# Layer 0's root as a power on GpSimd, for two channel blocks at a time, with order lists for it

## The chip, the cores and the metric

The kernel runs on one core of one Trainium2 chip. The metric is the device time of one execution in microseconds (us); a lower time is better. Engines are named as in the profile: PE (TensorE matmuls), PEld (its weight loads), DVE (VectorE), ACT (ScalarE), POOL (GpSimd), SP (the engine that only issues DMAs here).

## What is computed

Two layers over 32 batches of 512 channels (C) by 1024 columns (N), in float32, with one 512 x 512 matrix `adj`:

```python
q = jnp.einsum('c,bcn->bn', wq, x); k = jnp.einsum('c,bcn->bn', wk, x)
scores = q[:, None, :] + k[:, :, None]
scores = jnp.where(scores > 0, scores, NEG_SLOPE * scores)
att = jax.nn.softmax(scores, axis=-1)
agg = jnp.einsum('bcn,bmn->bcm', x, att)
out = jax.nn.relu(jnp.einsum('oc,bcm->bom', wm, agg) + bm[None, :, None])   # wm = adj
x = _layernorm(x + out, axis=-1)                       # layer 0: (x - m) / sqrt(v + 1e-5)
x = _layernorm(x + einsum('bnf,nm->bmf', x, adj) + bias, axis=-1)           # layer 1
```

## The kernel before

**Attention without the score matrix.** A score depends only on q + k. The kernel ranks the 1024 values of q (`rk`, a comparison with a count, on DVE), counts for each k how many q lie above the threshold (`ct`, a Sign with a sum, on ACT), forms z = adj x (`z`, on PE), scatters the rows of z to DRAM in the order of q (`sc`, indirect DMAs of POOL), loads them back (`sl`, SP), weights them with exponentials (`se`, ACT) and makes running sums from both ends (`u` and `d`, DVE; carries over partitions by `cu`, `cd` on PE, copied by `uc`, `dc` on ACT, added by `tu`, `td` on DVE). That table is written to DRAM (`tw`, `tl`, SP) and each column gathers its row of it (`g`, indirect DMAs of POOL). `mw` (DVE), `ms` (ACT) and `mx` (DVE) mix the two halves of a row; `t` turns the result by PE transposes into channels by columns.

**Layer 0's norm.** The 512 channels are four blocks of 128 partitions. For each block `r` (DVE, line 490) adds relu and residual into `x` with a row sum, and `s0` (ACT, line 468, a Square with a sum) gives the sum of squared deviations. Then one root for all four blocks: `rt` (`root0`, line 500) is a Sqrt on ACT over 128 x 4 values, and `rce` (`root0_end`, line 504) a reciprocal on DVE. `n0` (ACT, line 508) scales each block by it.

**Layer 1** multiplies by adj² + I in a Strassen-like form with seven half-size products: `U`, `V`, `Y`, `Z`, `11`, `12`, `21` (PE, lines 538, 540, 575) for two row groups each, on the sums `t1` to `t4` (DVE). `U` reads blocks 0 and 1 of `x` alone; `11` reads blocks 2 and 3. `Uc`, `Vc`, `Zc`, `ll` (ACT) and `up`, `lr` (DVE) take the products from PSUM; `s1`, `r1`, `n`, `st` are the second norm and the store. `r1` calls `root` (lines 475 and 476), which is on POOL: a multiply-add and a power of -0.5 over 128 x 1 values, followed by line 625.

**Order.** Nothing is scheduled by the compiler. Three lists of words give every engine its order: `head` (once), `loop` (once for each of 14 batches) and `tail` (once). A word is operation, batch relative to the list's base, and block: `rk.-1.5` is ranking of column block 5 of the batch before the base. `emit` (line 657) calls the functions in the order of the words; each engine keeps its own instructions in that order and waits by semaphores. So a word that waits holds up all later words of its engine. `pool_ops` and `pool_last` (lines 654 to 662) make `scatter` put a small memset on POOL between two scatters that follow each other.

**Buffers that tie batches together.** `tab` (the table) and `got` (gathered rows) have one buffer each, `sorted_z` and `table` in DRAM two each, `x` four. `zt`, from which the scatters read, has one, and `t3`, `t4` write into its column blocks 0 to 3. PSUM has four one-bank and two two-bank buffers.

Of the kernel before, what the change touches and what calls it, by code (L numbers as in the profile page):

```python
# [38 lines left out]
AF = mybir.ActivationFunctionType  # L39
# [10 lines left out]
def adj_resnorm_kernel(  # L50
# [447 lines left out]
    def root0(b):  # L498
            v = st[b].v0
            nc.scalar.activation(v[1], v[1], AF.Sqrt, scale=1.0 / N**3, bias=eps)  # L500

    def root0_end(b):
            v = st[b].v0
            nc.vector.reciprocal(v[1], v[1])  # L504
    
# [129 lines left out]
    def store(b, m):  # L635
# [12 lines left out]
        "ms": mix_scale, "mx": mix, "t": turn, "r": residual, "s0": spread0, "rt": root0, "rce": root0_end,  # L648
# [5 lines left out]
    pool_ops = ("sc", "g", "r1")  # L654
# [10 lines left out]
    bias.0 ld.1 ld.2 ld.3 pa.0 z.0.0 pc.0 co.0 zc.0.0 z.0.1 cc.0 ro.0 zc.0.1 pa.1 rc.0 ct.0.1  # L665
    rk.0.1 z.0.2 ct.0.3 rk.0.7 pc.1 rk.0.2 ct.0.5 z.0.4 rk.0.3 ct.0.2 rk.0.4 ct.0.7 rk.0.6 z.0.6
    zc.0.4 zc.0.2 rk.0.0 rk.0.5 co.1 zc.0.6 z.0.5 re.0 cc.1 ct.0.4 oq.0 sc.0.1 sc.0.6 z.0.3
    sc.0.0 zc.0.5 ct.0.6 sc.0.5 sc.0.2 z.0.7 zc.0.3 sc.0.4 ct.0.0 sc.0.3 ro.1 zc.0.7 sc.0.7
    z.1.0 rc.1 rk.1.3 ct.1.6 ct.1.5 rk.1.1 z.1.6 sl.0.0 sl.0.1 rk.1.7 rk.1.5 z.1.2 zc.1.6 rk.1.6
    ct.1.4 rk.1.0 zc.1.0 se.0.0 oq.1 rk.1.2 z.1.4 se.0.1 u.0.0 ct.1.1 ce.0 u.0.1 u.0.2 z.1.1  # L670
    rk.1.4 u.0.3 u.0.4 z.1.5 u.0.5 zc.1.1 zc.1.4 u.0.6 ct.1.3 u.0.7 zc.1.2 ct.1.7 d.0.7 pa.3
    d.0.6 zc.1.5 re.1 d.0.5 sc.1.1 cu.0 pc.3 d.0.4 ct.1.2 sc.1.5 co.3 z.1.3 d.0.3 uc.0 sc.1.2
    cc.3 d.0.2 ct.1.0 tu.0.0 sc.1.0 sc.1.4 z.1.7 d.0.1 zc.1.3 te.0 sc.1.3 d.0.0 tl.0 tu.0.1
    sc.1.6 cd.0 ro.3 dc.0 zc.1.7 pa.2 td.0.0 sc.1.7 z.2.5 rc.3 tw.0.0 rk.3.0 ct.3.0 ct.3.6
    td.0.1 z.2.0 zc.2.5 ct.3.3 ce.1 tw.0.1 rk.3.6 pc.2 ct.3.1 co.2 z.2.4 rk.3.3 ct.3.2 rk.3.1
    ct.3.4 rk.3.4 ct.3.5 z.2.3 cc.2 rk.3.7 zc.2.0 ct.3.7 rk.3.5 g.0.0 sl.1.0 zc.2.4 sl.1.1 ro.2
    rk.3.2 g.0.3 z.2.6 rc.2 g.0.1 ct.2.4 rk.2.2 zc.2.3 z.2.7 rk.2.6 ct.2.0 rk.2.1 we.0 se.1.0
    ct.2.3 rk.2.5 z.2.1 g.0.2 u.1.0 ce.3 g.0.4 u.1.1 oq.2 u.1.2 g.0.6 se.1.1 zc.2.6 rk.2.0 z.2.2
    zc.2.7 g.0.5 ct.2.7 rk.2.3 g.0.7 mw.0.0 rk.2.4 z.3.0 ms.0.2 ms.0.1 mx.0.2 ms.0.0 rk.2.7
    zc.2.1 ms.0.3 ct.2.1 u.1.3 z.3.4 re.2 mx.0.0 sc.2.6 ct.2.2 mw.0.1 sc.2.5 mx.0.1 ms.0.6  # L680
    mx.0.3 we.1 ms.0.5 z.3.1 sc.2.7 mx.0.6 ms.0.7 mx.0.5 ms.0.4 sc.2.4 mx.0.7 zc.2.2 mx.0.4
    sc.2.0 u.1.4 t.0.3 u.1.5 sc.2.3 t.0.1 r.0.3 sc.2.2 zc.3.4 r.0.1 s0.0.3 t.0.2 sc.2.1 u.1.6
    s0.0.1 t.0.0 r.0.2 z.3.2 u.1.7 s0.0.2 r.0.0 zc.3.0 zc.3.1 d.1.7 s0.0.0 cu.1 d.1.6 z.3.3 oq.3
    zc.3.2 d.1.5 uc.1 d.1.4 rt.0 d.1.3 re.3 d.1.2 z.3.5 zc.3.3 rce.0 d.1.1 n0.0.1 sc.3.3 d.1.0
    n0.0.0 sc.3.1 tu.1.0 n0.0.3 cd.1 sc.3.2 t1.0 U.0.0 dc.1 sc.3.0 zc.3.5 td.1.0 n0.0.2 sc.3.5
    U.0.1 ct.2.6 tu.1.1 tw.1.0 Uc.0.0 11.0.0 ct.2.5 td.1.1 11.0.1 Z.0.0 t2.0 tw.1.1 ce.2 V.0.0
    t3.0 Zc.0.0 we.3 t4.0 12.0.0 Uc.0.1 te.1 Vc.0.0 V.0.1 up.0.0 Z.0.1 Vc.0.1 s1.0.0 sl.2.0 tl.1
    Y.0.1 Zc.0.1 sl.2.1 12.0.1 lr.0.1 Y.0.0 up.0.1 se.2.0 g.1.0 u.2.0 21.0.1 lr.0.0 g.1.3 u.2.1
    21.0.0 se.2.1 g.1.1 u.2.2 ll.0.1 s1.0.1 g.1.2 u.2.3 z.3.6 ld.4 u.2.4 ll.0.0 r1.0.1 u.2.5
    ls.0.0 u.2.6 ls.0.1 u.2.7 r1.0.0 s1.0.3 cu.2 d.2.7 zc.3.6 d.2.6 z.3.7 uc.2 mw.1.0 g.1.7  # L690
    d.2.5 ms.1.0 tu.2.0 ms.1.2 g.1.5 n.0.1 g.1.6 pa.4 d.2.4 s1.0.2 tu.2.1 g.1.4 ms.1.3 z.4.5
    n.0.0 sc.3.6 mx.1.0 zc.3.7 r1.0.3 ms.1.1 d.2.3 pc.4 mx.1.2 d.2.2 co.4 z.4.4 mw.1.1 sc.3.4
    d.2.1 ms.1.7 r1.0.2 mx.1.1 ms.1.4 cc.4 ms.1.6 d.2.0 ms.1.5 ro.4 mx.1.4 zc.4.5 mx.1.6 cd.2
    sc.3.7 n.0.2 mx.1.5 z.4.0 mx.1.7 dc.2 st.0.2 rc.4 st.0.0 st.0.1 mx.1.3 ct.4.1 td.2.0 t.1.3
    zc.4.4 ct.4.6 t.1.1 r.1.3 tw.2.0 n.0.3 z.4.1 td.2.1 ct.4.4 zc.4.0 ct.4.5 r.1.1 tw.2.1 t.1.2
    st.0.3 ct.4.2 te.2 t.1.0 rk.4.6 s0.1.1 z.4.2 r.1.2 s0.1.3 r.1.0 s0.1.2 z.4.3 rk.4.4 s0.1.0
    rk.4.0 rt.1 rk.4.1 sl.3.0 tl.2 z.4.7 zc.4.3 sl.3.1 rce.1 rk.4.2 n0.1.1 rk.4.3 zc.4.1 n0.1.0
    rk.4.7 z.4.6 zc.4.2 se.3.0 g.2.0 rk.4.5 g.2.1 t1.1 n0.1.3 U.1.1 g.2.3 u.3.0 n0.1.2 u.3.1
    g.2.2 11.1.1 u.3.2 Uc.1.1 se.3.1 g.2.5 oq.4 u.3.3 we.2 ct.4.3 11.1.0 re.4 g.2.6 u.3.4 zc.4.7
    t2.1 ct.4.0 g.2.4 Z.1.0 u.3.5 ct.4.7 g.2.7 u.3.6 U.1.0 Zc.1.0 sc.4.3 u.3.7 mw.2.0 sc.4.5  # L700
    Z.1.1 d.3.7 ms.2.2 ce.4 sc.4.0 ms.2.1 d.3.6 ms.2.3 12.1.0 mx.2.2 sc.4.1 Zc.1.1 d.3.5 Uc.1.0
    mw.2.1 V.1.0 sc.4.2 d.3.4 ms.2.7 mx.2.1 zc.4.6 V.1.1 Vc.1.0 mx.2.7 up.1.0 12.1.1 Vc.1.1 t3.1
    s1.1.0 up.1.1 Y.1.0 ms.2.5 r1.1.0 ms.2.4 t4.1 ms.2.6 Y.1.1 ms.2.0 lr.1.0 s1.1.1 mx.2.4
    21.1.0 lr.1.1 r1.1.1 mx.2.0 21.1.1 d.3.3 mx.2.6 mx.2.5 cu.3 sc.4.6 ll.1.1 ld.5 d.3.2 n.1.0
    mx.2.3 d.3.1 ll.1.0 t.2.3 uc.3 ls.1.1 ls.1.0 d.3.0 t.2.2 s1.1.2 r.2.3 cd.3 r1.1.2 r.2.2
    t.2.0 dc.3 s1.1.3 tu.3.0 t.2.1 sc.4.7 n.1.2 r.2.0 pa.5 sc.4.4 s0.2.3 st.1.2 td.3.0 st.1.0
    r1.1.3 pc.5 s0.2.2 co.5 r.2.1 z.5.0 tw.3.0 cc.5 s0.2.1 td.3.1 s0.2.0 ro.5 tu.3.1 rt.2 z.5.2
    n.1.1 rc.5 tw.3.1 n.1.3 st.1.1 rce.2 te.3 z.5.1 n0.2.2 rk.5.6 tl.3 st.1.3 n0.2.3 rk.5.5
    n0.2.0 rk.5.3 11.2.0 ct.5.1 rk.5.7 n0.2.1 11.2.1 sl.4.0 rk.5.4 sl.4.1 ct.5.3 U.2.1 g.3.0
    t1.2 zc.5.0 we.4 g.3.2 rk.5.1 U.2.0 g.3.3 rk.5.0 Uc.2.1 ct.5.6 g.3.1 Z.2.0 t2.2 se.4.0  # L710
    zc.5.2 g.3.6 u.4.0 V.2.1 u.4.1 Zc.2.0 g.3.5 ct.5.4 rk.5.2 Z.2.1 g.3.7 Uc.2.0 u.4.2 re.5
    g.3.4 u.4.3 se.4.1 V.2.0 Zc.2.1 oq.5 u.4.4 ct.5.2 sc.5.0 u.4.5 12.2.1 mw.3.0 u.4.6 ms.3.1
    z.5.3 zc.5.1 u.4.7 Vc.2.1 sc.5.1 mx.3.1 ct.5.7 d.4.7 sc.5.2 up.2.1 12.2.0 zc.5.3 d.4.6
    ms.3.3 sc.5.3 mw.3.1 Vc.2.0 z.5.4 up.2.0 ms.3.5 ms.3.0 mx.3.5 ct.5.5 mx.3.3 ms.3.6 t3.2
    ms.3.7 s1.2.0 mx.3.6 Y.2.0 t4.2 zc.5.4 r1.2.0 ms.3.2 mx.3.7 Y.2.1 ms.3.4 lr.2.0 mx.3.2
    21.2.0 mx.3.4 n.2.0 mx.3.0 lr.2.1 t.3.1 s1.2.1 d.4.5 21.2.1 ll.2.0 r.3.1 r1.2.1 ct.5.0 d.4.4
    t.3.0 ld.6 ll.2.1 ls.2.0 d.4.3 t.3.2 s1.2.2 sc.5.4 d.4.2 cu.4 n.2.1 ls.2.1 r1.2.2 r.3.0
    z.5.5 uc.4 st.2.1 d.4.1 st.2.0 s1.2.3 d.4.0 n.2.2 r.3.2 cd.4 st.2.2 tu.4.0 t.3.3 dc.4 s0.3.2
    z.5.6 r.3.3 zc.5.5 s0.3.1 td.4.0 sc.5.5 s0.3.0 pa.6 td.4.1 tw.4.0 s0.3.3 z.5.7 zc.5.6 rt.3
    sc.5.6 r1.2.3 pc.6 rce.3 n0.3.1 co.6 n0.3.0 cc.6 tu.4.1 ro.6 n0.3.3 U.3.0 n0.3.2 t1.3 tw.4.1  # L720
    U.3.1 Uc.3.0 rc.6 zc.5.7 n.2.3 sc.5.7 t2.3 11.3.1 ct.6.2 st.2.3 rk.6.1 Uc.3.1 Z.3.1 ct.6.4
    t3.3 rk.6.3 ct.6.0 V.3.1 ct.6.5 ce.5 te.4 11.3.0 rk.6.0 Vc.3.1 tl.4 sl.5.0 Zc.3.1 sl.5.1
    Z.3.0 oq.6 t4.3 g.4.0 rk.6.6 V.3.0 Zc.3.0 ct.6.6 g.4.6 rk.6.4 12.3.1 Vc.3.0 g.4.2 rk.6.2
    se.5.0 g.4.1 12.3.0 u.5.0 g.4.3 u.5.1 Y.3.0 g.4.4 rk.6.7 z.6.1 g.4.5 up.3.0 g.4.7 up.3.1
# [238 lines left out]
```

## Time and profile before

| what | value |
|---|---|
| median of 3 runs | 2062.61 us (2061.65 to 2064.26) |
| profiled execution: time, span of its instructions | 2065.32 us, 2063.6 us |
| PE busy | 2004.7 us, 97% of the span |
| DVE, ACT, POOL busy | 1674.9, 1496.3, 874.6 us (81, 73, 42%) |
| granted TensorE clock, mean | 0.991 |
| line 500 on ACT: table loads, Sqrt | 31 x 1283 ns, 32 x 297 ns |
| line 298 on ACT: table loads ahead of the Exp | 26 x 1283 ns |
| line 504 on DVE, reciprocal of 128 x 4 | 32 x 177 ns (median) |
| lines 475 and 476 on POOL, 128 x 1 (mean) | 362 and 743 ns |

Busy time counts when an engine works, not whether the work sets the end. A matmul's end is modelled and overlaps the next one's start, so PE's pace is read from the distance of starts: 47 matmuls of `z` (128 x 512 outputs each) fill 20.33 us in the timeline, 0.43 us each.

### The profile page before, as it was taken

The page shows a single profiled execution, that of the slowest core. Times are in us where ns is not written, and L with a number is a line of the kernel's source. Part 1 is how long each engine was busy: PE and PEld are TensorE (multiplying, and loading weights), DVE is VectorE, ACT ScalarE, POOL GpSimd, SP SyncE. Part 2 cuts the span into 40 slices and gives each one's busy share as a digit, 9 for nine tenths or more (in the row PEclk, how much of TensorE's full clock was granted, in tenths as well). Part 3 has the DMA queues.
Part 4 walks back from the last instruction along what each step waited for, and adds up shares of the span by engine and source line. Part 5 has one row for each costly group of instructions (what it writes and reads, how often), then busy time and mean ns, then how long its engine had stood idle before and what let it go on. Part 6 is the DMA issues. An engine that isn't in the chain of part 4 may idle for free. (4 is left out here: it accounts for less than half of the span.)

```text
span 2063.6 us, 22066 instructions
## 1 busy us (share of the span) xinstructions
PE 2004.7 (97%) x6609; PEld 956.7 (46%) x6609; DVE 1674.9 (81%) x2778; ACT 1496.3 (73%) x2560; POOL 874.6 (42%) x1106
## 2 busy tenths in 40 slices
PE   8999999999999999999999999999999999999976
PEld 4444444444444444444444544444444444444432
DVE  6888898798877889887889888789778888789672
ACT  3566787678776777777777777777777777767566
POOL 4344543344343444443444443453444443443421
PEclk9999999999999999999999999999999999999988
DMA  5558776866667766667766767766677766677752
GB/s 226 212 222 312 275 287 266 306 264 257 271 245 291 307 255 246 271 266 292 306 241 250 273 268 296 290 249 258 255 276 306 276 244 268 245 269 273 286 204 82
DMA packets 137967, 541.04 MB, mean 262 GB/s; under 512 B 14404, under 2 KB 14416, under 8 KB 129656
## 3 DMA queue, kind: packets, MB, share of 16 engines
q1 hardware_dynamic: 80464, 337.47, 41.2%
q0 software_dynamic: 57344, 202.15, 26.0%
q8 instruction: 52, 0.85, 0.2%
q14 instruction: 67, 0.55, 0.1%
q10 hardware_dynamic: 40, 0.02, 0.0%
HBM read 270.29 MB, written 269.29 MB: 261 GB/s over the span
## 5 line engine op out<-in xcount | busy, mean ns | idle before, releaser
L310 PE MATMUL z_ps<-adj_t,x 128*128 128x512 f32 x2048 | 906.6, 593 | 0.4 <-ACT zt L316 0.4
L310 PEld LDWEIGHTS z_ps<-adj_t,x 128*128 128x128 f32 x2048 | 384.1, 190 | 448.0 <-issue 439.5
L324 POOL DMA_INDIRECT sorted_z<-zt,to x256 | 377.2, 1473 | 481.0 <-ACT zt L316 403.7
L432 POOL DMA_INDIRECT got<-table,of x256 | 262.2, 1024 | 209.6 <-issue 87.8
L271 DVE SCALAR_TENSOR_TENSOR junk_v<-qb,qkc,tie 128x1024 uint8<-128x1024 f32 x256 | 328.2, 1282 | 4.0
L284 ACT ACTIVATE junk_s<-qb,qkc 128x1024 bf16<-128x1024 f32 x256 | 293.9, 1148 | 18.9 <-DVE qb L261 17.0
L475 POOL TENSOR_SCALAR var<-var 128x1 f32<-128x1 f32 x128 | 46.3, 362 | 461.9 <-ACT junk L468 458.6
L454 ACT ACTIVATE got<-got,w 128x512 f32<-128x512 f32 x256 | 172.2, 713 | 64.2 <-DVE w L449 56.6
L316 ACT COPY zt<-z_ps 128x512 f32<-128x512 f32 x256 | 144.4, 577 | 68.4 <-PE z_ps L310 63.2
L459 DVE SCALAR_TENSOR_TENSOR got<-got,w 128x512 f32<-128x512 f32 x256 | 180.9, 745 | 10.9 <-ACT got L454 10.7
L490 DVE SCALAR_TENSOR_TENSOR x<-agg_ps,nbm,x 128x1024 f32<-128x1024 f32 x128 | 161.4, 1280 | 23.1 <-PE agg_ps L482 22.7
L372 DVE SCALAR_TENSOR_TENSOR tab<-tab,ac 128x513 f32<-128x513 f32 x224 | 168.0, 750 | 3.0
L631 ACT ACTIVATE g<-g,nb,var 128x1024 f32<-128x1024 f32 x128 | 157.8, 1238 | 11.8 <-POOL nb L625 11.8
L468 ACT ACTIVATE junk<-g,tot 128x1024 bf16<-128x1024 f32 x128 | 146.6, 1146 | 21.3 <-DVE g L595 16.8
L362 DVE SCALAR_TENSOR_TENSOR tab<-tab,ac 128x514 f32<-128x514 f32 x192 | 144.5, 752 | 16.9 <-ACT ac L348 11.7
L468 ACT ACTIVATE junk<-x,tot 128x1024 bf16<-128x1024 f32 x128 | 146.8, 1147 | 13.6 <-DVE x L490 8.3
L405 DVE TENSOR_TENSOR tab<-tab,carry 128x2052 f32<-128x2052 f32 x64 | 144.8, 2292 | 11.5 <-ACT carry L387 11.5
L540 PE MATMUL sum_ps<-x,adj 128*128 128x512 f32 x256 | 131.4, 637 | 16.3 <-ACT x L508 16.3
L482 PE MATMUL agg_ps<-ident,got 128*128 128x128 f32 x1024 | 133.4, 278 | 11.2 <-issue 4.7
L508 ACT ACTIVATE x<-x,var 128x1024 f32<-128x1024 f32 x128 | 138.5, 1149 | 0.7 <-DVE var L504 0.6
L601 DVE SCALAR_TENSOR_TENSOR g<-sum_ps,g 128x512 f32<-128x512 f32 x64 | 44.0, 687 | 111.8 <-ACT junk_s L284 75.3
L482 PEld LDWEIGHTS agg_ps<-ident,got 128*128 128x128 f32 x1024 | 115.2, 143 | 36.3 <-DVE x L490 12.2
(121 smaller groups left out, 2698.8 us busy)
## 6 DMA issues: line engine op xcount, KB each, us to landing
table<-tab SPq DMA_DIRECT2D x64, 2056.0 KB
tab<-sorted_z SPq DMA_DIRECT2D x64, 1028.0 KB
x<-in_x_dram SPq DMA_DIRECT2D x128, 512.0 KB
out_dram<-g SPq DMA_DIRECT2D x128, 512.0 KB
sorted_z<-zt,to POOLq DMA_INDIRECT x256
got<-table,of POOLq DMA_INDIRECT x256
adj_in<-in_adj_dram SPq DMA_DIRECT2D x1, 1024.0 KB
table<-end SPq DMA_DIRECT2D x32, 2.0 KB
```

Source lines behind the costliest of these rows:

```text
L271: nc.vector.scalar_tensor_tensor(junk, s.qb, s.q[:, j : j + 1], tie[:, at : at + N], ALU.subtract, ALU.is_gt, accum_out=s.rank[:, j : j + 1],)
L284: nc.scalar.activation(junk, s.qb, AF.Sign, bias=s.k[:, j : j + 1], accum_out=s.sign[:, j : j + 1])
L310: nc.tensor.matmul(s.z[j], xt[:, c, j * P : (j + 1) * P], adj_t[:, c, :], start=(c == 0), stop=(c == CT - 1),)
L324: nc.gpsimd.indirect_dma_start(out=sorted_z[b % 2][:, :], out_offset=bass.IndirectOffsetOnAxis(ap=s.to[:, j : j + 1], axis=0), in_=zt[:, j ...
L372: nc.vector.scalar_tensor_tensor(v, v, c, s.zs[:, j + 1, 0:D], ALU.mult, ALU.add)
L432: nc.gpsimd.indirect_dma_start(out=s.got[:, j, :], out_offset=None, in_=table[b % 2][:, :], in_offset=bass.IndirectOffsetOnAxis(ap=s.of[:, ...
L454: nc.scalar.activation(down, down, AF.Copy, scale=s.w[:, 1, j : j + 1])
L459: nc.vector.scalar_tensor_tensor(up, up, s.w[:, 0, j : j + 1], down, ALU.mult, ALU.add)
L468: nc.scalar.activation(junk, t, AF.Square, bias=v[0][:, i : i + 1], scale=-float(N), accum_out=v[1][:, i : i + 1],)
L482: nc.tensor.transpose(s.agg[o][:, j * P : (j + 1) * P], s.got[:, j, o * P : (o + 1) * P], ident)
L490: nc.vector.scalar_tensor_tensor(t[:, o, :], s.agg[o], nbm[:, o : o + 1], t[:, o, :], ALU.max, ALU.add, accum_out=s.v0[0][:, o : o + 1],)
L631: nc.scalar.activation(g, g, AF.Identity, bias=s.nb[:, m : m + 1], scale=s.v1[1][:, m : m + 1])
```

## The change

The root of layer 0's norm leaves ACT and DVE. `rt` now takes a half, h = 0 for blocks 0 and 1 or h = 1 for blocks 2 and 3, and calls the `root` that layer 1 has: two POOL instructions over 128 x 2 values. `rce` is gone. There are 64 words `rt` in place of 32 `rt` and 32 `rce`; all other words are the same, 5600 in all, but all three lists are new in their order. The loop begins at another point of the cycle, so `head` reaches one batch further and the loop still runs 14 times. `rt` joins the operations that reset the memset rule of POOL.

```diff
-    def root0(b):
-            v = st[b].v0
-            nc.scalar.activation(v[1], v[1], AF.Sqrt, scale=1.0 / N**3, bias=eps)
-
-    def root0_end(b):
-            v = st[b].v0
-            nc.vector.reciprocal(v[1], v[1])
-    
+    def root0(b, h):
+        root(st[b].v0, slice(2 * h, 2 * h + 2))
+
...
-        "ms": mix_scale, "mx": mix, "t": turn, "r": residual, "s0": spread0, "rt": root0, "rce": root0_end,
+        "ms": mix_scale, "mx": mix, "t": turn, "r": residual, "s0": spread0, "rt": root0,
...
-    pool_ops = ("sc", "g", "r1")
+    pool_ops = ("sc", "g", "r1", "rt")
...
-    for b in range(12, B - 6):
+    for b in range(13, B - 5):
```

Of the lists, the part of the loop around the root (before, then after):

```diff
-    r.-3.1 pa.0 uc.-2 r.-3.3 sc.-1.0 t.-3.0 pc.0 n.-4.2 d.-2.2 co.0 r1.-4.3 t.-3.2 te.-2 s0.-3.3
-    st.-4.2 d.-2.1 z.-1.4 r.-3.2 s0.-3.1 sc.-1.2 cc.0 r.-3.0 s0.-3.2 sc.-1.3 tu.-2.0 z.-1.5
-    s0.-3.0 sc.-1.1 zc.-1.4 d.-2.0 n.-4.3 sc.-1.4 tu.-2.1 rt.-3 st.-4.3 cd.-2 z.-1.6 dc.-2
-    rce.-3 zc.-1.5 td.-2.0 n0.-3.1 sc.-1.5 n0.-3.2
...
+    d.-2.3 r1.-4.3 r.-3.1 s0.-3.0 t.-3.2 n.-4.0 tu.-2.0 z.-1.3 zc.-1.2 st.-4.0 pc.0 r.-3.2
+    sc.-1.2 d.-2.2 sc.-1.0 co.0 zc.-1.3 z.-1.4 cc.0 d.-2.1 n.-4.1 sc.-1.3 te.-2 s0.-3.1 st.-4.1
+    d.-2.0 st.-4.2 tu.-2.1 n.-4.3 rt.-3.0 cd.-2 st.-4.3 t.-3.3 dc.-2 tl.-2 zc.-1.4 ro.0 td.-2.1
+    s0.-3.2 sc.-1.4 z.-1.7 r.-3.3 tw.-2.1 rc.0 s0.-3.3 z.-1.5 td.-2.0 n0.-3.1 rt.-3.1 ct.0.6
+    rk.0.0 tw.-2.0 n0.-3.0 z.-1.6 rk.0.3 zc.-1.5 we.-2 sc.-1.5 n0.-3.2 rk.0.7 rk.0.2 U.-3.1
```

The last root of the tail (batch 31 is -1), before and after:

```diff
-    mx.-1.5 s1.-2.2 up.-2.1 t.-1.1 ll.-2.1 s1.-2.1 t.-1.3 r.-1.1 r1.-2.1 r.-1.3 s0.-1.1 t.-1.0
-    r.-1.0 s0.-1.3 t.-1.2 r1.-2.2 r.-1.2 s0.-1.0 ls.-2.1 s0.-1.2 r1.-2.0 rt.-1 s1.-2.3 rce.-1
-    n0.-1.1 r1.-2.3 n0.-1.0 n.-2.0 t1.-1 U.-1.1 n0.-1.3 st.-2.0 U.-1.0 n0.-1.2 t2.-1 11.-1.0
...
+    mx.-1.7 n.-2.0 ls.-2.0 t.-1.0 up.-2.1 s1.-2.2 st.-2.0 r.-1.0 t.-1.1 s1.-2.1 r.-1.1 t.-1.3
+    s0.-1.0 r1.-2.1 r.-1.3 s0.-1.1 t.-1.2 Y.-2.1 r.-1.2 s0.-1.3 rt.-1.0 s0.-1.2 lr.-2.1 21.-2.1
+    n0.-1.1 rt.-1.1 n0.-1.0 ll.-2.1 r1.-2.2 U.-1.1 t1.-1 n0.-1.2 n0.-1.3 U.-1.0 n.-2.2 t2.-1
```

The stretch of the tail where batch 31's table is finished (-1) and batch 30's residual is made (-2), before and after:

```diff
-    d.-1.0 t.-2.0 tu.-1.0 s1.-3.1 st.-3.2 t.-2.1 cd.-1 r1.-3.1 r.-2.0 n.-3.0 dc.-1 ls.-3.1
-    r.-2.1 t.-2.2 s0.-2.0 td.-1.0 t.-2.3 n.-3.1 s0.-2.1 st.-3.1 r.-2.2 tw.-1.0 tl.-1 r.-2.3
-    s0.-2.2 td.-1.1 s0.-2.3 rt.-2 tu.-1.1 s1.-3.3 rce.-2 tw.-1.1 r1.-3.3 n0.-2.0 st.-3.0 n0.-2.1
...
+    td.-1.1 t.-2.0 n.-3.2 t.-2.1 st.-3.2 r.-2.0 tw.-1.1 r.-2.1 t.-2.2 s0.-2.0 tu.-1.0 s0.-2.1
+    t.-2.3 n.-3.3 rt.-2.0 td.-1.0 r.-2.2 n0.-2.0 tw.-1.0 r.-2.3 s0.-2.2 te.-1 s0.-2.3 tl.-1
+    st.-3.3 n0.-2.1 rt.-2.1 st.-3.1 U.-2.1 t1.-2 n0.-2.3 U.-2.0 g.-1.0 n0.-2.2 g.-1.2 t2.-2
```

And in the head, where batch 1's gathered rows are turned (`t.1`), before and after:

```diff
-    n.0.0 sc.3.6 mx.1.0 zc.3.7 r1.0.3 ms.1.1 d.2.3 pc.4 mx.1.2 d.2.2 co.4 z.4.4 mw.1.1 sc.3.4
-    d.2.1 ms.1.7 r1.0.2 mx.1.1 ms.1.4 cc.4 ms.1.6 d.2.0 ms.1.5 ro.4 mx.1.4 zc.4.5 mx.1.6 cd.2
-    sc.3.7 n.0.2 mx.1.5 z.4.0 mx.1.7 dc.2 st.0.2 rc.4 st.0.0 st.0.1 mx.1.3 ct.4.1 td.2.0 t.1.3
...
+    mx.1.7 r1.0.1 ms.1.0 mx.1.6 uc.2 ls.0.1 pa.4 mx.1.0 ms.1.5 d.2.2 sc.3.4 mx.1.5 n.0.1 z.4.4
+    mx.1.2 sc.3.6 n.0.0 d.2.1 st.0.1 mx.1.4 pc.4 st.0.0 s1.0.3 d.2.0 tu.2.1 t.1.1 r1.0.3 co.4
+    cd.2 cc.4 r.1.1 t.1.0 dc.2 zc.4.4 sc.3.7 r.1.0 n.0.3 t.1.3 z.4.0 td.2.1 st.0.3 s0.1.0 s0.1.1
```

## Prediction

> **What bounds the kernel now.** I read the page's busy shares and slices first.
>
> ```profile
> PE 2004.7 (97%) x6609; PEld 956.7 (46%) x6609; DVE 1674.9 (81%) x2778; ACT 1496.3 (73%) x2560; POOL 874.6 (42%) x1106
> ...
> PE   8999999999999999999999999999999999999976
> ...
> PEclk9999999999999999999999999999999999999988
> ```
>
> PE is full in 38 of 40 slices; its clock falls only in the last two. The busy time by stretch says how much is left (stretch, its length, then busy us of PE, PEld, DVE, ACT, POOL, the clock, DMA share, GB/s):
>
> ```profile
> 0.00:60.00 60.00, 51.44 (x197) 25.19 (x198) 40.14 (x76) 23.88 (x43) 25.40 (x38) 1.00 0.60 228
> ...
> 130.00:200.00 70.00, 66.48 (x215) 31.29 (x214) 54.54 (x79) 43.63 (x76) 32.73 (x32) 0.98 0.74 286
> ...
> 500.00:1700.00 1200.00, 1196.38 (x3956) 571.88 (x3955) 997.70 (x1657) 899.45 (x1537) 526.57 (x653) 1.00 0.69 271
> ...
> 1960.00:2000.00 40.00, 26.45 (x74) 13.54 (x73) 27.21 (x33) 26.46 (x39) 15.15 (x20) 0.79 0.57 220
> 2000.00:2040.00 40.00, 33.29 (x96) 15.07 (x95) 20.53 (x39) 28.80 (x44) 4.03 (x12) 0.91 0.24 97
> 2040.00:2063.60 23.60, 11.28 (x26) 4.47 (x24) 4.18 (x10) 11.45 (x17) 4.02 (x12) 0.81 0.22 89
> ```
>
> In 1200 us of loop PE is idle for 3.6 us. In the last 104 us it is idle for 32.6. The page Perfetto Trace Analysis of the Trainium skill (Identifying the Most-Contended Engine) calls matmul busy share a poor measure, because matmuls overlap; so I checked starts: `z` matmuls follow each other at 0.43 us, transposes at 0.11, and a loop period of 62.2 us (starts of `row`) holds about 60.9 us of such distances. What is above them is mostly changes of operand, and some 0.4 us of `t` waiting for the last `mx`. The loop is PE's and has no slack to give; only the ends have. PE's waits after 1880 us:
>
> ```profile
> PE sum_ps L540 <- ACT x L508: 16.3, 3, 8.8
> ```
>
> Those are `U` waiting for `n0` of batches 29, 30 and 31, so the root stands on this path there and nowhere else.
>
> **What the change removes.** The groups of the root:
>
> ```profile
> L476 POOL TENSOR_TENSOR var<-var,power 128x1 f32<-128x1 f32 x128 | 95.2, 743 | 10.7
> ...
> L475 POOL TENSOR_SCALAR var<-var 128x1 f32<-128x1 f32 x128 | 46.3, 362 | 461.9 <-ACT junk L468 458.6
> ...
> L500 ACT ACT_TABLE_LOAD x31 | 39.8, 1283 | 0.5
> ...
> L298 ACT ACT_TABLE_LOAD x26 | 33.4, 1283 | 0.4
> ...
> L500 ACT ACTIVATE var<-var,eps 128x4 f32<-128x4 f32 x32 | 9.5, 298 | 0.4
> ...
> L504 DVE RECIPROCAL var<-var 128x4 f32<-128x4 f32 x32 | 5.6, 176 | 13.4 <-ACT var L500 13.0
> ```
>
> The page ScalarE: Activation LUTs (What ACT_TABLE_LOAD costs) gives 1283 ns for a load, and a drain of about 1380 ns with it. The trace agrees on the load to the ns and shows no drain: below, the Sqrt starts 0.02 us after its load ends. Sqrt and Exp take turns, so each brings the other's load back: 31 + 26 + 4 (line 348) loads, of which one stays. ACT loses 60 x 1.28 + 9.5 = 86 us, DVE 5.6. That all loads go with Sqrt I take as given: no other pair of functions causes one now.
>
> **What it adds.** 64 pairs on POOL. The trace has only 128 x 1; two columns can't cost less than the fastest (0.18 + 0.55 us) nor more than two single ones (2 x 1.10 mean), so 0.73 to 2.2 us a pair; I take 1.15, 74 us in all, on an engine that is idle for 58% of the time. The spread is real (0.55 to 2.67 us for the power); GPSIMD Engine Reference (Key points) says that POOL shares its SBUF interfaces with DVE, which fits the slow ones lying beside busy DVE. No DMA is added; each moved word takes its DMAs with it on SP and POOL.
>
> **In the loop I cost this at nothing.** What covers it: counting PE's work along the new list, `rt.0` stands 9.4 us of PE work ahead of `n0.1`, and `n0.0` 3.4 us ahead of `U`; `rt.1` stands 3.5 us ahead of `n0.2`, and `n0.3` 2.3 us ahead of `11`. Queued behind a waiting `rt.1` on POOL are the next batch's scatters from block 5 on; but `zc.5`, which they need, comes 4 us later still. Before, `rt` had 4.3 us to `n0` and 4.3 from there to `U`, and PE did not wait. ACT's 2.7 us a period becomes idle time, since PE sets the period. The gathers stand 14 us ahead of `mw` in place of 8.5, and all but one `mx` 3 us ahead of `t`, so some of the 0.4 us may go: I take -2 us over some 20 periods, from -7 to +5.
>
> **In the tail it pays.** The path of batch 31 in the profile before, ACT first, then DVE, then POOL:
>
> ```profile
> 1979.32 1.28 ACT L500 ACT_TABLE_LOAD   x1
> 1980.62 0.30 ACT L500 ACTIVATE var<-var,eps 128x4 f32<-128x4 f32 x1
> ...
> 2019.75 0.30 ACT L500 ACTIVATE var<-var,eps 128x4 f32<-128x4 f32 x1
> ```
>
> ```profile
> 1980.02 2.29 DVE L405 TENSOR_TENSOR tab<-tab 128x2052 f32<-128x2052 f32 x1
> 1982.23 0.17 DVE L504 RECIPROCAL var<-var 128x4 f32<-128x4 f32 x1
> ```
>
> ```profile
> 1989.40 1.85 POOL L432 DMA_INDIRECT got<-table,of  x1 [6.04 <-DMA table<-tab]
> ```
>
> DVE works without pause from 1953 until the last table add ends at 1982.2; then write (7.2 us), gathers, mix (last `mx` 2011.7), four residuals, four `s0` (until 2019.7), Sqrt, reciprocal, two `n0`, and `U`'s real matmuls at 2023.3.
>
> Step a, DVE: between `mw.30.0` and the last table add of batch 31 the new list has all the same words but `te.31` (0.7), `up.29.0` (1.2), `lr.29.0` (0.7) and the residuals of blocks 2 and 3 (2 x 1.28): -5.2 us. `mw.30.0` needs the fifth gather in place of the fourth: +1.3. The table is ready at 1978.3, -3.9.
>
> Step b: the gathers start at 1985.5 and the last `mx` is done at 2007.8. PE can't take `t.31` sooner than its own work allows: `U.30.1` stays near 1983.4 (residual 3 now ends at 1980.8, then `s0` and one `n0`), and 22.6 us of products lie between, plus 2.5 at half clock, so 2008.5. Both arrive together.
>
> Step c: `U` reads blocks 0 and 1, whose root is now done beside `s0` of 3 and 2. From the last `s0` to the first `n0` there were 1.4 us (Sqrt, reciprocal, an `s1`); now none. `U.31.1` at 2018.2 in place of 2023.3: -5.1.
>
> Step d: `Y.30.1` and `21.30.1` (3.4 us) are moved into this gap, which shrinks from 6.2 us of idle time to pieces of about 1.3. TensorE: Matmul & The Clock Gate (What's actually happening) has the clock halved after an idle window of about 3.4 us; the trace agrees: the clock was 0.58 from 2023 to 2028, after that gap, which cost 2.1 us. That goes: -2.1. `12.31.1` now stands between `Y.31.1` and `21.31.1`, where PE waited 0.95 us for `lr`: -0.9. At the very end `s1.31.1` falls ahead of `ll.31.1`: +0.6. Tail: -5.1 - 2.1 - 0.9 + 0.6 = -7.5, from -10 to -3 (only the 1.4 of step c and half of d).
>
> **In the head it costs.** Before, PE waited 3.4 us at 176 us (`co.4`, behind ACT's wait for gathers) and then ran at half clock (1.7). Now `t.1.1`, the first word that needs all of batch 1's mix, stands after 161 us of PE work in place of 170. Its data is not earlier: `t.0` comes 10 us later, so DVE's residuals and with them batch 1's last table add end near 147 in place of 143.7, and gathers start near 163 (160.05 before). Eight gathers without a `r1` between them save 4 us, so `mw.1.1` stays near 180 and the last `mx` near 187. PE arrives at 176 and waits 11 us, plus 2.3 at half clock, against 5.1: +8. Later waits between 229 and 350 us (4.7 us in all) came from PE running ahead of DVE, and shrink: -5. Head: +3, from -2 to +9.
>
> **The sum.** -7.5 - 2 + 3 = -6.5 us on the profiled execution's 2065.3 (span 2063.6), which lies 2.7 above the median of 2062.6: 2056.
>
> **Rivals.** (1) The freed ACT time helps the loop too, and `t`'s wait ends: 22 periods x 0.35 = 7.7 in place of 2, giving 2050. For it speaks the longer lead of gathers and `mx`; against it that PE waits so little. (2) The head's wait is not given back, and the table of batch 31 is no earlier, so that the tail gives only its lower bound: +8 - 3 - 2 = +3, 2065.6. For it speaks that every step of the head's path is a wait seen before; against it that DVE set the pace there and PE's place in its list then matters little. (3) Slower: POOL's order. If `s0.3` slips in the loop by more than the 4 us that `zc.5` leaves, `rt.1` holds the scatters of blocks 5 to 7, and the table load behind them, which already ends waits of ACT line 348 (67.5 us in 34 times). Each us beyond 4 then lengthens 20 periods; it decides from 0.55 us a period (+11 against -6.5). At 0.7 it gives 2070. Against it: ACT has 2.7 us more room than before, and POOL waits for ACT 404 us at the scatters today.
>
> **How the numbers follow.** A change of under 0.2% (4.1 us) can hardly be told from none here. The forecast has 0.55 (2056, own range 2051 to 2061), rival 1 0.18, rival 2 0.16, rival 3 0.11. Faster than 2058.5: 0.8 of the forecast, all of rival 1, a little of 2: 0.64. Slower than 2066.7: 0.11. The rest, 0.25, lies between. The range 2047 to 2066 leaves out rival 3 and the far ends of rivals 1 and 2.
>
> **What would show it.** Right: one or two table loads; PE idle under 5 us from 500 to 1700; batch 31's first gather 3 to 5 us nearer to the end of its PE work, and no half clock after the last root; a PE wait of some 10 us near 176. Wrong: PE idle in every period with POOL named, or a tail whose last gather is no earlier against batch 31's last `z`.

## The result and the profile after

The changed kernel takes **2058.46 us** (median of 18 runs, 2055.18 to 2061.96); the kernel before, in 18 runs on the same chip, 2062.90 (2060.07 to 2066.96). The ratio is 0.998, with a 95% interval of 0.9973 to 0.9987: 4.4 us, about 0.2%. The same kernel measured twice more as a base of the experiments gave 0.9962 (0.9949 to 0.9976) and 0.9987 (0.9981 to 0.9994), so the three measurements give a gain of 4.4, 7.8 and 2.6 us, and what differs from one to the next is about as large as the gain.

The profiled execution took 2055.65 us (span 2053.8). It is one of the quickest, as that of before (2065.32) is one of the slower ones: the two profiles are 9.7 us apart, the medians 4.4. So a profile shows here where time went; how much of it is in an ordinary run the medians say.

From the page after, PE's busy share, its slices and its clock:

```profile
PE 2003.1 (98%) x6609; PEld 956.0 (47%) x6609; DVE 1673.3 (81%) x2746; ACT 1405.8 (68%) x2467; POOL 1029.1 (50%) x1182
...
PE   8999999999999999999999999999999999999967
...
PEclk9999999999999999999999999999999999999989
```

ACT lost 90.5 us, GpSimd (POOL) gained 154.5. The half clock is in one slice instead of two. The busy time by stretch (stretch, length, busy us of PE, PEld, DVE, ACT and POOL, clock, DMA share, GB/s):

```profile
130.00:200.00 70.00, 63.86 (x225) 31.15 (x224) 55.60 (x79) 44.09 (x77) 33.45 (x38) 0.93 0.71 271
...
500.00:1700.00 1200.00, 1200.00 (x3971) 573.77 (x3970) 1003.13 (x1646) 847.10 (x1489) 636.32 (x698) 1.00 0.71 274
1960.00:2000.00 40.00, 27.58 (x75) 13.66 (x76) 28.83 (x39) 25.30 (x37) 22.69 (x24) 0.75 0.68 264
2000.00:2040.00 40.00, 38.34 (x111) 17.37 (x110) 19.05 (x35) 29.02 (x44) 7.89 (x19) 1.00 0.13 53
```

PE has no idle time at all in 1200 us of loop (3.6 before). From 2000 to 2040 it is busy for 38.3 us in place of 33.3, at full clock in place of 0.91. From 130 to 200 it is busy for 63.9 in place of 66.5: the head got worse. The groups of the root, shapes kept apart:

```profile
L475 POOL TENSOR_SCALAR var<-var 128x2 f32<-128x2 f32 x64 | 86.8, 1356 | 85.4 <-ACT junk L468 84.5
L476 POOL TENSOR_TENSOR var<-var,power 128x2 f32<-128x2 f32 x64 | 78.0, 1218 | 5.3
...
L163 ACT ACT_TABLE_LOAD x1 | 1.3, 1283 | 4.5 <-DVE zero L137 4.5
```

One table load is left. A pair of the root takes 1.36 + 1.22 = 2.57 us.

To add up the waits of PE by place I took, from the trace, every distance between the starts of two matmuls that is over 0.13 us above what that kind takes when nothing waits (0.43 us for 512 columns, 0.11 for a transpose). Half clock is in it. Differences of the sum agree with differences of the spans within about 2 us:

| kernel (its profiled time) | to 300 us | 300 to 480 | 480 to 1700 | 1700 to 1920 | from 1920 | sum |
|---|---|---|---|---|---|---|
| before (2065.3) | 12.6 | 2.6 | 4.6 | 2.4 | 32.8 | 54.9 |
| after (2055.7) | 21.3 | 0 | 0 | 0.3 | 24.6 | 46.2 |

So in the profiles the tail gives 8.2, the loop 6.7, and the head costs 6.1. PE's waits in the tail, from 1880 us on:

```profile
PE carry_ps_False L380 <- ACT junk L468: 9.0, 1, 9.0
PE sum_ps L535 <- ACT x L503: 5.6, 2, 4.2
```

The 16.3 us of `U` for three batches are 5.6 for batch 30 alone; a wait of 9.0 us stands at `cd.31` instead. The profile puts it down to ACT, but what `cd.31` reads is DVE's last `d` of batch 31, which ends at 1965.5, 0.1 us before the matmul starts. The columns of a timeline line are start, duration, engine, line, operation, and what was waited for. The path of batch 31, first DVE's last table add, then the first gather, then ACT's last `s0` and the first `n0`:

```profile
1974.38 2.29 DVE L405 TENSOR_TENSOR tab<-tab,carry 128x2052 f32<-128x2052 f32 x1
```

```profile
1984.00 1.05 POOL L432 DMA_INDIRECT got<-table,of  x1 [2.11 <-DVE x L514]
```

```profile
2012.29 1.15 ACT L468 ACTIVATE junk<-x,tot 128x1024 bf16<-128x1024 f32 x1
2013.35 0.19 ACT L468 ACTIVATION_READ_ACCUMULATOR junk<-x,tot 128x1 f32 x1
2013.44 2.17 ACT L503 ACTIVATE x<-x,var 128x1024 f32<-128x1024 f32 x2
```

`n0` starts when the last `s0` ends, `U` of batch 31 follows at 2015.7 (its small bias matmul at 2015.2), and from the end of `t.31` to its last matmul at 2040.9 PE has one wait of more than 0.2 us, of 0.95.

### The profile page after: what moved, and what is told of

The parts are those of the page before. It is cut to its first block, busy times and chain, and to the rows that moved or that the text cites. A ratio compares the mean times of both kernels' runs of the same rounds, so it can differ in the third digit from the quotient of the medians.

```text
span 2053.8 us, 22188 instructions
## 1 busy us (share of the span) xinstructions
PE 2003.1 (98%) x6609; PEld 956.0 (47%) x6609; DVE 1673.3 (81%) x2746; ACT 1405.8 (68%) x2467; POOL 1029.1 (50%) x1182
## 4 chain that ended last, share of the span: by engine, by line
PE 91%; DVE 3%; ACT 2%; DMA 2%; issue 1%; POOL 1%; SPq 0%; ACTq 0%; DVEq 0%; POOLq 0%
PE z_ps L310 41%; PE sum_ps L535 21%; PE pair_ps L535 11%; PE pair_ps L570 5%; PE agg_ps L482 5%; PE qk_ps L221 3%; PE q_tp L252 1%; PE carry_ps_False L380 1%; PE carry_ps_True L380 1%; DMA x<-in_x_dram 1%; PE pair_ps L533 1%; PE sum_ps L533 1%; ACT junk L468 1%; DVE tab L405 1%; DVE junk_v L271 0%
## 5 line engine op out<-in xcount | busy, mean ns | idle before, releaser
L324 POOL DMA_INDIRECT sorted_z<-zt,to x256 | 352.9, 1378 | 284.1 <-ACT zt L316 166.4
L475 POOL TENSOR_SCALAR var<-var 128x1 f32<-128x1 f32 (+1 forms) x192 | 144.4, 752 | 567.9 <-ACT junk L468 563.0
L490 DVE SCALAR_TENSOR_TENSOR x<-agg_ps,nbm,x 128x1024 f32<-128x1024 f32 x128 | 162.9, 1278 | 37.3 <-PE agg_ps L482 37.1
L476 POOL TENSOR_TENSOR var<-var,power 128x1 f32<-128x1 f32 (+1 forms) x192 | 180.1, 938 | 16.0
L503 ACT ACTIVATE x<-x,var 128x1024 f32<-128x1024 f32 x128 | 144.9, 1143 | 18.7 <-POOL var L476 18.5
L590 DVE SCALAR_TENSOR_TENSOR g<-pair_ps,g 128x1024 f32<-128x1024 f32 x64 | 78.2, 1221 | 82.8 <-PE pair_ps L535 60.4
```

The source lines that it names most:

```text
L324: nc.gpsimd.indirect_dma_start(out=sorted_z[b % 2][:, :], out_offset=bass.IndirectOffsetOnAxis(ap=s.to[:, j : j + 1], axis=0), in_=zt[:, j ...
L476: nc.gpsimd.tensor_tensor(v[1][:, at], v[1][:, at], power[:, at], ALU.pow)
```

## The experiments

All were timed against the kernel before on their own chip, so they are compared by their ratio to it. The sums of PE's waits, as above, each from one profiled execution:

| kernel | ratio, interval | to 300 | 300 to 480 | 480 to 1700 | 1700 to 1920 | from 1920 |
|---|---|---|---|---|---|---|
| changed, again | 0.9962 (0.9949, 0.9976) | 19.5 | 0 | 0 | 0 | 25.1 |
| changed, third time | 0.9987 (0.9981, 0.9994) | 21.0 | 0 | 0 | 0 | 25.2 |
| operation alone | 1.0127 (1.0107, 1.0146) | 13.1 | 3.6 | 29.5 | 3.6 | 33.7 |
| operation moved up | 1.0166 (1.0136, 1.0196) | 13.7 | 5.2 | 30.0 | 7.8 | 34.0 |
| order alone | 0.9986 (0.9979, 0.9994) | 23.7 | 0 | 3.5 | 1.6 | 24.8 |
| loads back | 0.9978 (0.9970, 0.9985) | 19.6 | 0 | 1.6 | 1.9 | 25.1 |
| new tail alone | 0.9985 (0.9977, 0.9994) | 12.0 | 3.6 | 2.2 | 4.6 | 25.7 |
| old tail | 1.0018 (1.0006, 1.0030) | 20.9 | 0 | 0 | 0 | 35.0 |
| old head | 0.9953 (0.9939, 0.9967) | 13.2 | 5.4 | 0 | 1.0 | 25.6 |
| old head with Sqrt | 0.9956 (0.9944, 0.9969) | 13.9 | 5.6 | 0.2 | 1.4 | 25.3 |
| root doubled | 1.0050 (1.0037, 1.0063) | 30.4 | 0 | 3.2 | 2.4 | 26.6 |
| root in one piece | 1.0123 (1.0108, 1.0138) | 29.8 | 1.0 | 12.3 | 2.1 | 29.6 |

**The changed kernel again.** 

> The changed kernel once more, as the base for the other three and for a second profile, since its single times spread over 7 us (2055 to 2062) around 2058.5 and the first profile (2055.65) is one of the quickest. Expected: 0.998 of the kernel before. Theory: an ordinary execution shows the same head and tail, and now and then the wait of `t` for the last `mx` in the loop, as the kernel before does, with some 3 us in all. Rival: the 3 us lie in the head or in the tail, so that one of the two gains read from the first profile is partly luck.

2057.88 us (2054.26 to 2062.27, 7 runs). Its profile came from its quickest run and again shows no wait in the loop; neither does the third one, of an execution of 2056.39. No profile is of one of the longer executions, so where those lose up to 8 us is open. One hint: in each of the three measurements of this kernel the executions with a mean granted clock of 0.988 or 0.989 took longer on average than those with 0.990 or 0.991 (2059.9 against 2057.7 us, 2060.7 against 2056.5, 2060.5 against 2057.9), so more time at half clock is part of it.

**Operation alone.** The lists of before; only this:

```diff
     def root0(b):
-            v = st[b].v0
-            nc.scalar.activation(v[1], v[1], AF.Sqrt, scale=1.0 / N**3, bias=eps)
+        for h in range(2):
+            root(st[b].v0, slice(2 * h, 2 * h + 2))
     def root0_end(b):
-            v = st[b].v0
-            nc.vector.reciprocal(v[1], v[1])
+        pass
-    pool_ops = ("sc", "g", "r1")
+    pool_ops = ("sc", "g", "r1", "rt")
```

> The order of the kernel before, with only the operation changed: the two pairs of columns of the root on GpSimd at the word `rt`, no Sqrt, no reciprocal. Theory (the order pays, the operation is hidden): ACT gives up 86 us of table loads that PE did not wait for; in the tail a load, a Sqrt and a reciprocal (1.76 us) are replaced by four GpSimd instructions (2.2 to 4.4 us), so 0 to +4 us, about 2064. Rival (the operation pays, the lists only follow it): ACT's 2.7 us a period end the waits of `t` and the tail gains, so about 2058, the whole of what the change brought.

2093.13 us, 27 us slower than before: outside both expectations. Of the 28.5 us that PE waits more, 24.9 lie between 480 and 1700; the waits from 500 to 1700 us:

```profile
PE sum_ps L539 <- ACT x L507: 23.2, 17, 1.8
```

`U` waits for `n0` in 17 periods. One of them, on POOL, then ACT, then DVE:

```profile
934.66 2.57 POOL L324 DMA_INDIRECT sorted_z<-zt,to  x1 [0.23 <-issue]
937.30 1.89 POOL L475 TENSOR_SCALAR var<-var 128x2 f32<-128x2 f32 x1
939.28 2.66 POOL L476 TENSOR_TENSOR var<-var,power 128x2 f32<-128x2 f32 x1
942.02 0.19 POOL L475 TENSOR_SCALAR var<-var 128x2 f32<-128x2 f32 x1
942.30 0.70 POOL L476 TENSOR_TENSOR var<-var,power 128x2 f32<-128x2 f32 x1
```

```profile
931.95 1.15 ACT L468 ACTIVATE junk<-x,tot 128x1024 bf16<-128x1024 f32 x1
...
941.97 4.28 ACT L507 ACTIVATE x<-x,var 128x1024 f32<-128x1024 f32 x4 [4.67 <-POOL var L476]
```

```profile
934.11 2.29 DVE L405 TENSOR_TENSOR tab<-tab 128x2052 f32<-128x2052 f32 x1
936.85 4.50 DVE L405 TENSOR_TENSOR tab<-tab,carry 128x2052 f32<-128x2052 f32 x2 [0.45 <-ACT carry L387]
```

The last `s0` ends at 933.1, the first `n0` starts 8.9 us later. In the kernel before, in the period around 927 us, this stretch is 4.2 us, and the root in it is a table load of 1.28, a Sqrt of 0.30 and a reciprocal of 0.18. The 8.9 us are two parts of about the same size: until 937.2 POOL is at scatters that stand ahead of the root, and the first pair then takes 4.6. Each of the first three POOL instructions shown ends 0.1 to 0.8 us after a table add of DVE does; the second pair, behind the adds, takes 0.19 + 0.70. Over this whole trace the power on two columns takes 2.71 us (median) beside a table add with the carry and 0.70 where DVE is idle. The Trainium skill, SBUF — State Buffer (Who interferes with whom), says that a VectorE instruction with two inputs in SBUF contends with a GpSimd instruction that reads SBUF, and calls such contention an exclusive lock. The traces agree: in the changed kernel's, a pair that lies beside `L490`, which has one of its inputs in PSUM, keeps its 0.19 and 0.72 us.

**Operation moved up.** As in operation alone, but `rt.b.h` stands right behind the later of the two `s0` of its half:

```diff
-... s0.15.2 sc.17.3 tu.16.0 z.17.5 s0.15.0 sc.17.1 ... sc.17.4 tu.16.1 rt.15
+... s0.15.2 rt.15.1 sc.17.3 tu.16.0 z.17.5 s0.15.0 rt.15.0 sc.17.1 ... sc.17.4 tu.16.1
```

> The old order with the root on GpSimd, as in the run that lost 27 us, but each pair of the root stands right behind the later of its two `s0`, ahead of the scatters that it stood behind. In that run's trace, at 933.1 us the last `s0` is done; GpSimd then does a scatter until 937.2, the first pair of the root until 941.9 (4.6 us, beside DVE's table add), and the first `n0` starts at 942.0. Theory (the place in GpSimd's queue is the loss): the first `n0` comes 4 us sooner or more, `U`'s wait of 1.0 to 1.8 us in each period goes, and the time falls to 0.997 to 1.000 of before. Rival (the length of the pair beside the table adds is the loss): the pairs move into the other table add, half of the loss stays, 1.004 to 1.008.

2093.32 us, no better (the profile is of a longer execution, 2100.04); both expectations fell, the theory's by most. POOL and DVE in one period:

```profile
938.25 1.57 POOL L475 TENSOR_SCALAR var<-var 128x2 f32<-128x2 f32 x1 [1.26 <-ACT junk L468]
939.90 1.12 POOL L476 TENSOR_TENSOR var<-var,power 128x2 f32<-128x2 f32 x1
941.21 2.37 POOL L324 DMA_INDIRECT sorted_z<-zt,to  x1 [0.20 <-issue]
943.66 1.89 POOL L475 TENSOR_SCALAR var<-var 128x2 f32<-128x2 f32 x1
945.63 2.66 POOL L476 TENSOR_TENSOR var<-var,power 128x2 f32<-128x2 f32 x1
```

```profile
938.01 1.76 DVE L405 TENSOR_TENSOR tab<-tab 128x1539 f32<-128x1539 f32 x1
...
940.35 2.29 DVE L405 TENSOR_TENSOR tab<-tab 128x2052 f32<-128x2052 f32 x1
943.20 4.50 DVE L405 TENSOR_TENSOR tab<-tab,carry 128x2052 f32<-128x2052 f32 x2 [0.56 <-ACT carry L387]
```

The run did not do what it was made for. In this order the half that `U` needs (blocks 0 and 1) is the second pair, and the scatter that I had wanted behind the root stands between the two. From the last `s0` (939.3) to the first `n0` (948.3) it is 9.0 us again: 4.3 for the rest of the other half's pair and the scatter, 4.6 for the pair itself. From 938 to 948 POOL does about one instruction for each table add of DVE, the scatter too. So both runs show that a root next to a row of table adds, with `n0` and `U` right behind, costs some 30 us; how much of it is the place in the queue and how much the longer pair is not settled.

**Order alone.** The new lists with Sqrt and reciprocal by halves:

```diff
     def root0(b, h):
-        root(st[b].v0, slice(2 * h, 2 * h + 2))
+        v = st[b].v0[1][:, 2 * h : 2 * h + 2]
+        nc.scalar.activation(v, v, AF.Sqrt, scale=1.0 / N**3, bias=eps)
+    def root0_end(b, h):
+        v = st[b].v0[1][:, 2 * h : 2 * h + 2]
+        nc.vector.reciprocal(v, v)
```

> The lists of the changed kernel, but the root by Sqrt on ACT and a reciprocal on DVE, for two blocks at a time at the words `rt` (the reciprocal one DVE word later), so the table loads come back, some 60 of them. Theory (the order pays): 2058.5 plus 1 to 2 us for the load and Sqrt in the tail, about 2060, faster than the kernel before. Rival (the operation pays): 2062 or more.

2061.46 us against 2057.88 for the changed kernel on the same chip and 2065.72 before: about half of that gain is there without the new operation. The changed kernel's other two ratios, 0.998 and 0.9987, are as good as the 0.9986 here, so by them all of it is. What the operation adds to the order is between nothing and 4 us. The tail is the same (24.8 against 25.1 of waits); the profile is of one of the longer executions (2065.74).

**Loads back.** The changed kernel with an unused Sqrt:

```diff
         root(st[b].v0, slice(2 * h, 2 * h + 2))
+        if h == 0:
+            nc.scalar.activation(look, eps[0:1, :], AF.Sqrt)
```

> The changed kernel with a Sqrt of a single element on ACT at each first half of the root, used by nobody: it brings the table loads back (two a batch, about 2.6 us of ACT), while the root stays on GpSimd. The new lists with the old Sqrt and reciprocal stood 3.6 us above the changed kernel (medians). Theory (ACT's time is hidden, as the prediction has it): 0 to 1 us above the changed kernel; the 3.6 us then belong to the chain Sqrt, reciprocal on DVE, norm. Rival: the loads are what those 3.6 us were: 3 to 4 us above.

0.9978, between the three ratios of the changed kernel. By the profile, PE waits 2 to 4 us more in all; from 480 to 1920, where the changed kernel has almost none, it waits 3.5. Two loads a batch are hidden but for about that; the two theories are not told apart.

**New tail alone, and old tail.** The lists are cut at word 4978 and go on with the words left over in the other kernel's order, with that kernel's root.

> The kernel before, with its Sqrt and its order up to word 4978 (batch 27's norm), then the changed kernel's order and root for the last four batches. It measures the tail's part alone. Theory: the steps a to d of the tail hold, 7 to 8 us under the kernel before (0.9963); the waits of `U` for the root of batch 31 and the half clock go. Rival: the tail's gain is only there behind the new loop, because DVE's backlog at the cut decides: then under 3 us.

> The reverse: the changed kernel up to word 4978, then the order and the Sqrt of before for the last four batches. Theory: what is left is the loop's gain (7 us of waits of `t` by the profiles) less the head's cost (5 to 6 us), so 0 to 3 us under the kernel before (0.999). Rival: loop and head bring nothing and the two results of this pair add up with all of it in the tail: 1.000 here and 0.996 for the new tail alone.

The new tail alone: 2061.98 us, 3 us under before; its interval, about 1 to 5 us, leaves out the 7 to 8 of the theory and is nearer to the rival. The old tail behind the new loop: 2069.42, 4 us above before, which neither expectation had, and 0.3 to 0.6% above the changed kernel. In the profiles the tail is worth 7.1 us (32.8 to 25.7) and 9.9 (25.1 to 35.0). The new tail alone has 4.6 us of waits around the cut in place of 2.4, which is the splice's own. With the old tail all three waits of `U` are back:

```profile
PE sum_ps L543 <- ACT x L511: 16.9, 3, 9.1
```

So the tail gives 3 us and what the splice costs by the one, 6 to 12 by the other. New head and new loop together give nothing: with the old tail the kernel is 1 to 6 us slower than before, and only 2.2 of that are waits in the tail that the kernel before does not have (35.0 against 32.8).

**Old head, on GpSimd and with Sqrt.** The first 1200 words (1195) in before's order, then the changed kernel's; the root on GpSimd throughout, or with Sqrt for batches 0 to 5.

> The changed kernel with the head of the old order: the first 1200 words (up to about 435 us of PE work, batch 6) in the order of before, the rest as in the changed kernel; the root on GpSimd throughout. By the two profiles the new head holds 6 us more of PE's waits up to 420 us. Theory: these 6 us come off, 2052 to 2053. Rival: a wait in the head is given back, because PE then runs ahead of DVE and waits for it later; then 2057 to 2059.

> The order of before with its Sqrt for batches 0 to 5 (1195 words), then the changed kernel's order and root on GpSimd. By the profiles PE waits 15 us in the head of before, 19 to 21 in the changed one, 18.5 in the old order with the root on GpSimd. Theory: the head's cost is real and comes off: 4 to 5 us under the changed kernel, 0.994 of before. Rival: PE's waits in the head are DVE's pace and return later: within 1 us of the changed kernel, 0.996.

2055.75 and 2056.31 us, 0.9953 and 0.9956, against 0.9962 for the changed kernel beside the first: within the intervals, and the first lies between what theory and rival had. The profile shows the rival at work. Up to 300 us the old head waits 13 to 14 us in place of 19 to 21; from 300 to 480, where the changed kernel has none, it waits 5.4 to 5.6. Of 6 us, 5 are given back. Both may be a little better than the changed kernel, which these runs can't tell.

**Root doubled.**

```diff
+        nc.gpsimd.tensor_scalar(twin, v[1][:, at], 1.0 / N**3, EPS, ALU.mult, ALU.add)
+        nc.gpsimd.tensor_tensor(twin, twin, power[:, at], ALU.pow)
         root(v, at)
```

> The changed kernel, as the base of the three that follow. So far its ratio to the kernel before was 0.998 and 0.996; expected 0.997.

> The changed kernel with each pair of the root done twice, the first time into a tile that nobody reads: 0.9 us more of GpSimd ahead of each half when DVE leaves it alone, up to 4.5 beside a table add. It measures the cover that the prediction counted: 9.4 and 3.4 us of PE work for the first half, 3.5 and 2.3 for the second. Theory (the cover is there): within 1 to 4 us of the changed kernel, at most 0.2 us a period. Rival (the cover is used up, since the second pair already takes 4 us beside a table add): `11` waits for `n0` in each period, 0.5 to 1 us, 10 to 20 us in all, 1.002 to 1.007 of before.

The changed kernel had 2059.29 us here, this one 2072.39: 13 us more: not the 1 to 4 of the theory, but not where the rival wanted them either:

```profile
500.00:1700.00 1200.00, 1197.93 (x3976) 573.49 (x3975) 999.09 (x1635) 843.72 (x1485) 719.68 (x774) 1.00 0.70 273
```

With 2.4 us more of POOL ahead of every half (L501 and L502: 78.5 + 78.0 us for 64), PE is idle for 2.1 us in 1200. As the pair that counts now often falls behind the table adds and is shorter, a half is done 2.0 us later on average, from the start of its first POOL instruction. The loop has nearly all of that cover: 3.2 and 2.4 us of waits from 480 to 1920 in place of none. The head has none: 30.4 us of waits in place of 21.0.

**Root in one piece.** The new lists, four columns at once at the word of the second half, the first two `n0` behind it:

```diff
-... td.16.0 n0.15.1 rt.15.1 ct.18.6 ...
+... td.16.0 rt.15.1 n0.15.1 ct.18.6 ...
-        root(st[b].v0, slice(2 * h, 2 * h + 2))
+        root(st[b].v0, slice(0, CT))
```

> The new lists with the root in one piece: one pair of GpSimd instructions on all four columns at the place of the second half, and the two first `n0` behind it (the first half's words and `n0` of batch 0 likewise, with its `U`). Theory (two blocks at a time are what the lists are built on): in the changed kernel's trace the second pair ends at 937.9, the first `n0` would start there in place of 933.8, and `U`, now at 940.9, would wait 0.5 to 1.2 us in each period: 1.002 to 1.008 of before. Rival (only the place in the queue counts, not the halves): `n0` is early enough all the same, and half the GpSimd instructions are gone: 0.997.

2086.61 us, 27 us above the changed kernel. From 500 to 1700 us:

```profile
PE sum_ps L535 <- ACT x L503: 11.0, 16, 0.7
```

`U` waits 0.7 us in 16 periods, as the theory had it; head (30.8) and tail (29.6) lose 10 and 4 us more, so that the whole, 1.0123, is above its 1.008.

## Why the prediction was right

2056 us with 2047 to 2066 was said, 2058.5 came. The 0.64 for faster meant a time under 2058.5, and 2058.46 lies on that line: on which side it fell was luck. The mechanism was the forecast's, a gain in the tail and a loop that hides the root; the terms were off by several us in both directions. (One reading was off too: PE's slices are at 9 in 37 of 40, not 38; the first is at 8.)

**Removed.** As said: 60 loads, the Sqrts and the reciprocals, one load left, 90 us off ACT. In the loop nearly nothing of it reaches PE (loads back: 2 to 4 us in all). **Added.** The price was wrong: a pair takes 2.57 us, not 1.15, and more than the upper bound of 2.2. The pairs that I scaled from, 128 x 1 at the places of `r1`, start beside a table add of DVE in 2 of 128 cases; of the new pairs 48 of 64 do. POOL's bill was 165 us, not 74. In the loop it did not matter to the time: the second pair takes up to 3.95 us there, less than the 3.5 + 2.3 us of cover that the prediction had counted, and the root doubled shows that the loop hides nearly all of 2 us more. In the head it did matter:

```profile
144.51 1.09 POOL L475 TENSOR_SCALAR var<-var 128x2 f32<-128x2 f32 x1 [2.20 <-ACT junk L468]
145.68 1.59 POOL L476 TENSOR_TENSOR var<-var,power 128x2 f32<-128x2 f32 x1
...
147.30 1.15 ACT L503 ACTIVATE x<-x,var 128x1024 f32<-128x1024 f32 x1 [2.90 <-POOL var L476]
```

The second pair of batch 0 takes 2.8 us, beside a table add and then `t1` on DVE; two `n0` follow it, and `11`, which reads them, starts at 149.6 after a wait of 3.0. With Sqrt and reciprocal in the same order (order alone) it waits 1.9 there. **Cost nothing in the loop**: held for these lists and for them alone. The third rival feared POOL's order, with a late root that holds up the scatters. What the old lists do with the new operation is near to it, but the other way round: scatters and DVE's table adds hold up the root, and `n0` and `U` are late, at some 1.3 us a period (29.5 - 4.6 over 19) and 27 us in all.

**Loop, -2.** In the profiles -6.7: `t`'s wait is gone in all three profiles of the changed kernel, as the first rival had it. But the old loop's waits vary: the new tail alone, which has the old loop, shows 2.2 us from 480 to 1700 us where before's profile shows 4.6. By the medians, with the old tail, loop and head together give nothing; they do not tell the loop from the head. With the head's cost, -2 fits the medians better than -7, which the quickest runs show.

**Tail, -7.5.** -8.2 in the two profiles, -7.1 and -9.9 in those of the spliced pair. Step a: the last table add ended at 1976.7 (1978.3 was said). Step b: first gather at 1984.0 (1985.5), last `mx` at 2004.7 (2007.8); but `U.30.1` did not stay at 1983.4. Its first two matmuls ran at 1978.5, behind the one `n0` that stands ahead of residual 3; only the other two waited for residual 3, its `s0` and an `n0`, as I had it for all four, until 1981.9. So `t.31` came at 2005.7 (2008.5). Step c: `U.31.1` at 2015.7 (2018.2), -7.6 in place of -5.1. The 1.4 between last `s0` and first `n0` went as said, but not because Sqrt and reciprocal left ACT and DVE: order alone has both, and its first `n0` starts when the last `s0` ends too. It is the root by halves that does it. Step d: the gap closed to pieces of 0.95 and 0.2 us (the wait for `lr` is in it now), and the half clock in it went (clock 1.00). What took its place is the wait of 9.0 us at `cd.31` for DVE: the idle time moved forward, as PE cannot outrun DVE's backlog. From the last matmul to the end it is 0.6 us longer, as said.

**Head, +3.** +6.1 up to 480 us. The one wait of 11 us at `t.1.1` did not come. The cost came in pieces: 3.0 at 146 us (`11` of batch 0) and 1.7 of half clock, some 4 us of `pa.4` waiting for its x load at 174 to 180 and 2.1 of half clock (13.3 was said for about this place), 2.5 at 229 and 1.8 of half clock, 1.9 at 277. Between 229 and 350 us the waits did not shrink by 5: they are 5.2 us before and 7.2, 5.0 and 5.2 in the three profiles. Only from 300 to 480 did they go (2.6 to 0). So the head is near to +3 because too much at 176 stands against a return that was too large and a wait at 146 that was left out.

**The sum.** -8.2 - 6.7 + 6.1 is -8.8 between two profiles; the medians say -4.4 in one measurement, -8 and -3 in the others. The sum of -6.5 was right within what can be told, with a tail of the right size in the profiles, and a loop and a head whose errors cancel; that they do is luck.

## What to carry to other kernels

Price a small GpSimd instruction by what DVE does at its new place, not by its mean elsewhere: beside a DVE instruction with two SBUF inputs it ended only after that one here. A root of four instructions that saves 86 us of ACT can cost 27 us if the lists leave it between the last statistics and the first use; here a root by halves, with other ACT work ahead of the second half, kept nearly all of it out of PE's way in the loop. Test an operation and its order apart before putting a gain down to either, and read its size from medians where the profiled runs sit at one end of the spread.

## What was not expected of the hardware

Three things. GpSimd's indirect DMAs are held up beside DVE's table adds, whose two inputs are in SBUF, as its arithmetic is: the scatters take 2.36 us (median) beside the table add with the carry and 0.97 with DVE idle, in the trace of the changed kernel. The power hardly depends on its columns when nothing interferes: 0.56 us for one, 0.70 for two. And waits of PE much shorter than the 3.4 us that the Trainium skill, TensorE: Matmul & The Clock Gate (What's actually happening), names for an idle window can bring the half clock: gaps of 1.9 us in the operation-alone kernel cost 1.7 us more at 752 and 1642 us and nothing at 880, 944, 1071, 1262 and 1452; of the changed kernel's gaps, 3.0 us at 146 cost 1.7 in the first profile and nothing in the third. The clock records of the traces fit a reading of this. In the operation-alone kernel half clock is granted from 754.39 to 757.80 and from 1645.27 to 1648.68: each time for 3.41 us, and the two starts are 261 such stretches apart, as on a fixed grid. The two gaps that cost time lie whole between two lines of that grid; each of the other five is cut by a line. The changed kernel's gap at 146 fits too: 2.5 and 3.0 us of it lie in one stretch of the grid in the first and second profile, which have the half clock there, and at most 2.1 in the third, which has not. So the same gap can be free in one execution and not in the next. That the grid decides is read from these gaps and was not tested.
